# Repeated rows of step sizes and products, loaded per unit or per pair, in a hybrid Mamba kernel

## The chip, the core and the metric

The kernel runs on one NeuronCore of one Trainium2 chip. The core has five engines that run their own instruction queues in order: TensorE (PE, matrix products, with its weight loads shown as PEld), VectorE (DVE), ScalarE (ACT), GpSimd (POOL) and SyncE (SP). Here SP computes nothing: it issues most of the DMA transfers, one after another, and waits in front of each one until its buffer and its data are ready. The transfers themselves run on 16 DMA engines of the core. SBUF is the on-chip memory of 128 partitions; DRAM here is the chip's external memory.

The metric is the device time of one execution in microseconds (us). The kernel before has a median of 1525.69 us over 3 runs (1517.64 to 1526.01).

## What is computed

Eight sequences of 512 tokens with 256 channels pass four layers, each with a residual around it: a Mamba block with a feed-forward part, a gated recurrence over the 8 sequences, attention, and the same recurrence again. The change lies in the Mamba block, in its scan over time. Cut to that, the reference is:

```python
delta = jax.nn.softplus(dbc[..., :dt_rank] @ dt_proj_w + dt_proj_b)
Bm = dbc[..., dt_rank:dt_rank + N]
Cm = dbc[..., dt_rank + N:]
A = -jnp.exp(A_log)
deltaA = jnp.exp(delta[..., None] * A)
BX = (delta * xc)[..., None] * Bm[:, :, None, :]
def step(h, inp):
    dA, bx, c = inp
    h = dA * h + bx
    return (h, jnp.einsum('ben,bn->be', h, c))
```

Each of the 256 channels has 16 states (N). So the step sizes `delta` (called dl in the kernel) and the products `delta * xc` (called dx) are needed 16 times over, once for each state.

## The kernel before

**Tiling of the scan.** SBUF has 128 partitions. They are filled with 16 states times 8 channels; that is a *unit* (`scan_unit`, L403). 256 channels make 32 units for each sequence b, and 8 sequences make 256 units. A unit goes through these steps, each named in the order texts by a short word:

- `dl` and `dx` (`load_unit`, L374): the 8 rows of 512 floats are read from DRAM and written 16 times, once for each state, into one half of a tile `dl_rep` or `dx_rep` of 128 x 2 x 512. One DMA of 256 KB each, in pieces of one row, 2048 bytes. The two units u and u+1 (u even) share a tile; three such tiles exist for dl and three for dx.
- `da` (`decay`, L389): ACT computes exp(A * dl) for one unit into PSUM.
- `bx` (`increments`, L396): POOL multiplies dx by the repeated B, for a pair of units at once.
- `sc` (L405): DVE runs the scan over the 512 tokens. `cm` (L411): DVE multiplies by the repeated C.
- `y` (`sum_states`, L414): PE sums the 16 states of four units, one matmul for each, into the 32-row block j of a bank.

**Where the rows come from.** The step sizes of a sequence are computed by ACT into an SBUF tile `dl` of 128 x 2 x 512 (channel = 128 k + partition), the products by POOL into `dx` (piece `i.dx`, L328; for the first sequence by DVE in two halves). Pieces `i.store_dl` and `i.store_dx` (`store`, L330) write them to a DRAM tile of shape (k, partition, token), 512 KB each. For the first sequence each half k is stored by itself. All these DMAs are issued by SP (`nc.sync`). `i.rows` (L309) loads the repeated B and C, 256 KB each.

**Order.** All order is written out by hand. The texts `FRONT`, `SLOTS` (used 7 times, once for each step from one sequence to the next), `LAST` and `REST` list words; `mamba_and_recurrence` (L870) walks through them, and each word emits the next piece of its kind: `dl` the next load of a unit, `sc` the next scan and so on; `i.` pieces belong to the input side of the next sequence, `o.` to the output side of the previous one, `q.` and `r.` to the recurrence. Each engine then executes its part of the list strictly in that order. Around the stores, `SLOTS` reads (L831, L832):

```
cm sc cm cm cm sc sc cm y dx o.down3 o.down2 dl i.store_dl i.store_dx dx dl dl dx dl dx q.output0
i.rows dl q.g1 da e.square q.output0_ sc cm sc dx dx sc cm cm sc o.add3 cm cm o.add2 bx bx r.stats
```

The loads run ahead of their use by the three buffers: at the stores, the loads of units 0 to 28 of the running sequence are out for dl; those of 29 to 31 and the first ones of the next sequence follow the stores on SP's queue.

**Unit numbers.** Unit u has half k = u // 16, row block j = u % 4 and r = (u // 4) % 4; its channels start at 128 k + 32 j + 8 r. So the two units of a pair lie 32 channels apart.

Of the kernel before, what the change touches and what calls it, by code (L numbers as in the profile page):

```python
# [9 lines left out]
F32 = mybir.dt.float32  # L10
# [5 lines left out]
P = 128  # L16
B = 8
L = 512
E = 256
KC = E // P  # L20
TC = L // P
NS = 16
CG = P // NS
UNITS = E // CG
QR = 4
HC = 8
KCONV = 4
R = 64
# [108 lines left out]
def load_a(cx, w):  # L137
# [23 lines left out]

    a.sum = pool.tile([P, QR, HP], F32, name="sum")
    nc.gpsimd.memset(a.sum, 0.0)
    for r in range(QR):
        nc.vector.tensor_reduce(
# [12 lines left out]
def mamba_in(cx, a, t, b):  # L178

    nc, v = cx.nc, cx.v  # L180
    n = f"a{b}"
# [147 lines left out]

    def store(what, k):  # L330
        if not k:
            d = cx.dram.tile([KC, P, L], F32, tag=what, name=f"{what}_dram_{n}")
            setattr(t, what + "_d", d)
        to, x = (
            y[:, chunk(k), :]
            for y in (getattr(t, what + "_d").rearrange("k p l -> p k l"), getattr(t, what))
        )
        nc.sync.dma_start(to, x)

    def chunk(k):  # L340
        return slice(0, KC) if k is None else slice(k, k + 1)

    pieces = {
        f.__name__: f
        for f in (
            stats, rms, outer, residual, silu_z, silu_x, xproj, xproj_, rows, take_c,
        )
    }
# [3 lines left out]
    for k in (None, 0, 1):  # L352
        on = "" if k is None else f".{k}"
        pieces["dx" + on] = lambda k=k: times_input(k)
        for what in ("dl", "dx"):
            pieces[f"store_{what}{on}"] = lambda what=what, k=k: store(what, k)
        if on:
            pieces["silu_x" + on] = lambda k=k: silu_xk(k)
    for name, f, count in (("turn", turn, KC), ("proj", proj, 2 * KC), ("conv", conv, KC), ("dt", dt, KC)):
# [5 lines left out]
    return pieces  # L365


def unit_channels(u):


    return u // 16, u % 4, u // 4 % 4


def load_unit(cx, t, b, u, what):  # L374

    k, j, r = unit_channels(u)
    pair = getattr(t, what + "_rep")
    if u % 2 == 0:
        pair[u // 2] = cx.rep.tile(
            [P, 2, L], F32, tag=what, bufs=3, name=f"{what}_rep_a{b}_{u}"  # L380
        )
    c0 = j * HP + r * CG
    src = getattr(t, what + "_d")[k, c0 : c0 + CG, :]
    cx.nc.sync.dma_start(
        pair[u // 2][:, u % 2, :], src.unsqueeze(0).to_broadcast([NS, CG, L])
    )


def decay(cx, a, t, b, u):  # L389
# [13 lines left out]
def scan_unit(cx, t, b, u):  # L403
    t.hc[u] = cx.scan.tile([P, L], F32, tag="hc", bufs=HC, name=f"hc_a{b}_{u}")
    cx.nc.vector.tensor_tensor_scan(  # L405
# [8 lines left out]
def sum_states(cx, a, t, b, quad):  # L414

    k, r = quad // QR, quad % QR
    if r == 0:
        t.y[k] = cx.psum.tile([P, L], F32, tag="y", bufs=1, name=f"y_a{b}_{k}")
        cx.nc.tensor.matmul(t.y[k], a.D[:, k, :], t.xc[:, k, :], start=True, stop=False)
    for j in range(4):  # L420
        cx.nc.tensor.matmul(  # L421
            t.y[k][head(j), :],
            a.sum[:, r, :],
            t.hc[4 * quad + j],
            start=False,
            stop=(r == QR - 1),
        )
# [391 lines left out]


SLOTS = """
dx q.i0_ a.take_c y q.g0 sc o.gate1 cm i.rms x.load sc sc q.g0_ dl dl dl dx dl dl dl dx dx dx dx dx
dl dl dx dx dl dx dl dx dx dl da i.scale o.proj0 dx dx dl dx dl q.update0 dl dl o.proj1 i.turn0 q.f1
o.add_proj o.stats i.turn1 q.i1 da i.turn0_ q.f1_ sc i.turn1_ o.norm q.i1_ da cm cm cm q.hold1 y
o.turn0 bx bx e.stats bx bx bx o.residual c.bias bx bx bx o.turn1 o.turn0_ da sc sc o.turn1_ da
i.proj1 o.up0 o.up2 o.up1 da i.proj1_ o.up0_ da o.up2_ o.up1_ da da i.proj0 o.up3 o.up3_ i.proj0_ da
da e.center da sc cm sc cm i.conv1 cm sc da sc cm cm o.down1 y sc i.proj3 o.down0 x.half sc i.proj2
cm o.add1 i.conv0 sc cm sc cm i.silu_x i.silu_z y da i.xproj da i.xproj_ o.up4 dx dl dl dl dl dx dl
dx dx dx dx dl sc dl dx cm sc cm cm cm sc y i.dt1 sc o.add0 i.dt0 o.up5 o.up6 o.up7 da o.up4_ da
e.affine i.dt1_ i.dt0_ bx bx bx da i.dx da o.up5_ da o.up6_ da da o.up7_ da da e.outer da c.gate0 sc  # L830
cm sc cm cm cm sc sc cm y dx o.down3 o.down2 dl i.store_dl i.store_dx dx dl dl dx dl dx q.output0  # L831
i.rows dl q.g1 da e.square q.output0_ sc cm sc dx dx sc cm cm sc o.add3 cm cm o.add2 bx bx r.stats  # L832
bx e.residual sc sc q.g1_ r.norm cm cm q.update1 q.output1 y da r.turn0 y r.turn1 r.turn0_ da
r.turn1_ da r.f0 sc sc r.f0_ cm x.first sc r.i0 dl dl dx dl dx dl cm sc cm cm r.hold0 dx x.spill bx
da da q.output1_ bx dl dx da
"""


LAST = """
da dl dx dx q.i0_ da da dl dx dx sc y o.gate1 o.proj0 o.proj1 q.g0 dx dl dl dl dx x.spill dl dx dl  # L840
q.f1 dl dx dl dx dl x.load dx dx q.i1 dl dx dx sc sc o.add_proj bx o.stats a.take_c sc q.g0_ o.norm
sc q.f1_ da cm q.update0 sc cm q.hold1 cm cm dx dl dl dx dl dl dl dx dx dx dl dx dx dl dx dl dl dl
dl dx dx dx dl o.turn1 dl dx dl dl dx o.turn0 y o.turn1_ o.turn0_ bx bx bx o.up0 da da bx o.residual
bx bx bx bx o.up3 o.up1 bx o.up4 o.up2 q.i1_ da o.up0_ da da da q.output1_ o.up3_ o.up1_ da da da
o.up2_ q.output0_ da da o.up4_ da r.output0_ cm sc cm sc sc cm sc cm cm cm sc y sc cm cm y o.down0
o.down1 o.up6 o.up5 o.up7 o.up6_ da da o.up5_ da o.up7_ da da sc sc cm cm sc sc sc o.add0 o.add1 sc
# [15 lines left out]
i.stats i.outer i.center.a i.affine.a i.center.b i.affine.b i.square.a i.square.b i.residual i.rms  # L862
i.scale.a i.scale.b i.turn0 i.turn1 i.turn0_ i.turn1_ i.proj0 i.proj1 i.proj0_ i.proj1_ i.conv0
i.conv1 e.stats i.silu_x.0 i.silu_x.1 i.proj3 i.xproj i.xproj_ i.dt0 i.dt1 i.proj2 i.dt0_ i.dt1_
e.center i.dx.0 i.dx.1 i.rows e.affine i.store_dl.0 i.store_dx.0 i.store_dx.1 dl dx dx e.outer dl dl
da dx i.store_dl.1 e.square bx da da dx dl dx dx dl e.residual bx i.silu_z dx dl dx
"""


def mamba_and_recurrence(cx, a, w, d):  # L870
    nc = cx.nc
    T = [Ctx() for _ in range(B)]
    parts = {}
# [24 lines left out]

    parts["x", 0] = {"half": half_gates, "first": lambda: first_bias(cx, d.s)}
    for b in (1, 2, 3):  # L900
        parts["x", b + 1] = {"spill": lambda b=b: spill(b)}
    for b in (5, 6, 7):
        parts.setdefault(("x", b - 2), {})["load"] = lambda b=b: take_over(b)

    each = {
        "dl": (UNITS, lambda b, n: load_unit(cx, T[b], b, n, "dl")),
        "dx": (UNITS, lambda b, n: load_unit(cx, T[b], b, n, "dx")),
        "da": (UNITS, lambda b, n: decay(cx, a, T[b], b, n)),
        "bx": (UNITS // 2, lambda b, n: increments(cx, T[b], b, n)),
        "sc": (UNITS, lambda b, n: scan_unit(cx, T[b], b, n)),  # L910
        "cm": (UNITS, lambda b, n: times_c(cx, T[b], n)),
        "y": (UNITS // 4, lambda b, n: sum_states(cx, a, T[b], b, n)),
    }
    done = dict.fromkeys(each, 0)

    def run(b, one):
        if "." in one:
            who, what = one.split(".", 1)
            if (who, b) in parts and what in parts[who, b]:
                parts[who, b][what]()  # L920
        else:
            count, f = each[one]
            at, n = divmod(done[one], count)
            if at < B and (one != "y" or 4 * done[one] + 4 <= done["cm"]):
                f(at, n)
# [627 lines left out]
def lay_out(i):  # L1553
# [3 lines left out]
    i = {k: np.asarray(v) for k, v in i.items()}  # L1557
    A, F, T = "L0_attn_a_", "L0_ffn_", "L0_attn_b_"
# [32 lines left out]
    for h in range(H):  # L1591
        r = h % (2 * HG) * DH
        m = h % HG * HP
        watt[h // (2 * HG), r : r + DH, m : m + DH] = i[T + "w_att_val"][h]

    a_log = i[A + "A_log"].reshape(KC, 4, QR, CG, NS).transpose(4, 3, 0, 2, 1).reshape(P, UNITS)
    vecs = [a_log if name == "A_log" else cols(i[vec[name]]) for name, _ in _VECS]
    return {
        "x": i[A + "x"],
# [40 lines left out]
```

## Time and profile before

The execution that the profiler recorded took 1520.85 us; its span from the first to the last instruction is 1519.1 us. It lies between the lowest and the highest of the three timed runs.

| | busy us | share of the span |
|---|---|---|
| PE (matmul) | 1437.2 | 95% |
| PEld (weight load) | 702.1 | 46% |
| DVE | 1086.7 | 72% |
| ACT | 836.0 | 55% |
| POOL | 501.0 | 33% |

| stretch | what runs | granted PE clock | DMA share |
|---|---|---|---|
| 0 to 40 us | loads, input side of sequence 0 | 0.98 | 0.70 |
| 40 to 110 us | scans of sequence 0 | 0.82 | 1.02 |
| 110 to 190 us | scans of sequence 1 | 0.91 | 1.02 |
| 190 to 650 us | scans of sequences 2 to 7 | 1.00 | 0.87 to 1.01 |
| 650 to 1519 us | end of the recurrence, attention, second recurrence | 0.90 to 1.00 | 0.12 to 0.16 |

The DMA share is the mean busy share of the 16 DMA engines; it can come out a little over 1, because records of packets overlap slightly. The two kinds of repeated loads are the bulk of all traffic: 512 DMAs of 256 KB, 134 MB of the 197 MB moved. An engine's share over the span says little by itself: the engines have different limits in different stretches, and idle time of an engine that nobody waits for costs nothing.

### The profile page before, as it was taken

What the parts mean: (1) busy time and instruction counts of PE and PEld (TensorE: products, weight loads), DVE (VectorE), ACT (ScalarE), POOL (GpSimd) and SP (SyncE); (2) the same over time, 40 slices, a digit from 0 to 9 for tenths busy, and PEclk for the clock granted to TensorE, in tenths of its full rate; (3) what the DMA queues carried; (4) which work ended last, traced back from release to release, by engine and by line L of the source; (5) the groups of instructions that cost most, each with busy time, mean ns of one, the idle gap of its engine ahead of it and who ended that gap; (6) DMA issues with size and microseconds to landing.
All of it is one profiled execution on the core that took longest, in us unless ns stands there. A gap on an engine that the chain in (4) does not pass through costs nothing.

```text
span 1519.1 us, 19714 instructions
## 1 busy us (share of the span) xinstructions
PE 1437.2 (95%) x6812; PEld 702.1 (46%) x6812; DVE 1086.7 (72%) x1628; ACT 836.0 (55%) x1283; POOL 501.0 (33%) x300
## 2 busy tenths in 40 slices
PE   4479999999999999999899999999999999999998
PEld 1125455655555555667334443334333333333347
DVE  4799999999999899833766767565656646555326
ACT  5666778676867665522255464645455444554522
POOL 2777777776768566512300000000000000000000
PEclk9699999999999999999799999999999999999999
DMA  7999999899999999703101100100110001110214
GB/s 233 265 260 247 266 241 281 235 265 258 258 260 254 238 253 266 203 1 114 56 19 45 41 17 23 37 19 15 37 23 26 22 15 34 23 37 8 79 68 139
DMA packets 112141, 196.77 MB, mean 130 GB/s; under 512 B 17201, under 2 KB 27761, under 8 KB 112041
## 3 DMA queue, kind: packets, MB, share of 16 engines
q1 hardware_dynamic: 109752, 188.52, 46.7%
q10 hardware_dynamic: 1824, 5.15, 1.0%
q0 software_dynamic: 464, 1.84, 0.3%
q8 instruction: 54, 0.88, 0.2%
q14 instruction: 47, 0.38, 0.1%
HBM read 163.24 MB, written 23.56 MB: 123 GB/s over the span
## 4 chain that ended last, share of the span: by engine, by line
PE 82%; DVE 10%; ACT 3%; issue 2%; DMA 2%; POOL 1%; SPq 0%; ACTq 0%; DVEq 0%; POOLq 0%
PE ps_e_c L1104 10%; PE ps_s_c L1104 10%; PE ps_o_c L1124 8%; PE ps_f_o L522 6%; PE ps_f_o L498 6%; DVE hc_a L405 3%; PE y_a L421 3%; PE ps_in_a L245 3%; PE ps_w_c L1204 2%; PE ps_f_d L599 2%; PE ps_i_d L599 2%; PE ps_g_d L599 2%; DVE hc_a L411 2%; PE ps_v_c L1070 2%; PE ps_f_d L612 2%
## 5 line engine op out<-in xcount | busy, mean ns | idle before, releaser
L1386 DVE TENSOR_REDUCE mp<-ps_s_c 128x2 f32<-128x1024 f32 x256 | 305.5, 1222 | 174.0 <-PE ps_s_c L1104 125.5
L1403 ACT ACTIVATE e_c<-ps_e_c 128x1024 f32<-128x1024 f32 x256 | 255.2, 1022 | 221.3 <-PE ps_e_c L1104 146.4
L398 POOL TENSOR_TENSOR bx_a<-dx_rep_a,B_a 128x1024 f32<-128x1024 f32 x128 | 301.5, 2368 | 107.0 <-DMA dx_rep_a<-dx_dram_a 55.7
L405 DVE TENSOR_TENSOR_SCAN hc_a<-da_a,bx_a 128x512 f32<-128x512 f32 x256 | 304.6, 1214 | 20.2 <-POOL bx_a L398 9.6
L391 ACT ACTIVATE da_a<-dl_rep_a,neg_a 128x512 f32<-128x512 f32 x256 | 173.7, 688 | 113.9 <-DMA dl_rep_a<-dl_dram_a 64.3
L1104 PE MATMUL ps_e_c<-q_c,keys 32*128 32x512 f32 x1024 | 226.3, 630 | 0.7 <-DVE q_c L1395 0.7
L1104 PE MATMUL ps_s_c<-keys,q_c 32*128 32x512 f32 x1024 | 223.1, 649 | 3.0 <-DVE mp L1386 1.7
L411 DVE TENSOR_TENSOR hc_a<-hc_a,Cp_a 128x512 f32<-128x512 f32 x256 | 164.6, 674 | 0.0
L85 POOL TENSOR_TENSOR rs_d<-ve_d,neg_half 128x4 f32<-128x4 f32 x8 | 8.1, 1015 | 404.1 <-DVE ve_d L84 212.9
L1124 PE MATMUL ps_o_c<-e_c,va 128*32 128x512 f32 x1024 | 135.5, 607 | 0.0
L498 PE MATMUL ps_f_o<-h_o,w 128*128 128x256 f32 x512 | 116.6, 381 | 1.3 <-ACT f_o L511 0.8
L1104 PEld LDWEIGHTS ps_e_c<-q_c,keys 32*128 32x128 f32 x1024 | 68.5, 183 | 101.4 <-issue 52.9
L522 PE MATMUL ps_f_o<-w,f_o 128*128 128x256 f32 x512 | 115.1, 381 | 0.0
L498 PEld LDWEIGHTS ps_f_o<-h_o,w 128*128 128x128 f32 x512 | 96.2, 190 | 28.6 <-ACT da_a L391 6.8
L522 PEld LDWEIGHTS ps_f_o<-w,f_o 128*128 128x128 f32 x512 | 96.4, 190 | 22.1 <-ACT da_a L391 5.0
L421 PE MATMUL y_a<-hc_a,sum 128*32 128x512 f32 x512 | 90.1, 625 | 15.5 <-DVE hc_a L411 15.5
L1104 PEld LDWEIGHTS ps_s_c<-keys,q_c 32*128 32x128 f32 x1024 | 65.8, 187 | 72.5 <-issue 29.9
L85 POOL TENSOR_TENSOR rs_c<-ve_c,neg_half 128x4 f32<-128x4 f32 x7 | 7.1, 1010 | 217.6 <-DVE ve_c L84 217.6
L511 ACT ACTIVATE f_o<-ps_f_o,vecs 128x256 f32<-128x256 f32 x128 | 53.0, 467 | 23.4 <-PE ps_f_o L498 23.4
L245 PE MATMUL ps_in_a<-hT_a,w_in 128*128 128x512 f32 x128 | 65.0, 638 | 0.4 <-ACT dl_a L307 0.4
L1124 PEld LDWEIGHTS ps_o_c<-e_c,va 128*32 128x32 f32 x1024 | 21.6, 108 | 89.6 <-issue 87.1
L115 PE MATMUL ps_hT_a<-ident,h_a 128*128 128x128 f32 x64 | 13.4, 332 | 37.0 <-ACT h_a L225 35.9
(317 smaller groups left out, 1974.8 us busy)
## 6 DMA issues: line engine op xcount, KB each, us to landing
dl_rep_a<-dl_dram_a SPq DMA_DIRECT2D x256, 256.0 KB
dx_rep_a<-dx_dram_a SPq DMA_DIRECT2D x256, 256.0 KB
x<-in_x_dram SPq DMA_DIRECT2D x8, 512.0 KB
keys<-xT_c SPq DMA_DIRECT2D x128, 32.0 KB
o_c<-oT_c SPq DMA_DIRECT2D x128, 32.0 KB
xT_dram_d<-xT_d SPq DMA_DIRECT2D x8, 512.0 KB
xT_back<-xT_dram_d SPq DMA_DIRECT2D x8, 512.0 KB
sum_c<-inverse_c SPq DMA_DIRECT2D x15, 256.0 KB
```

Source lines behind the costliest of these rows:

```text
L245: nc.tensor.matmul(ps, a.in_proj[:, k, ts(m, P)], t.hT[:, k, :], start=(k == 0), stop=(k == KC - 1))
L391: cx.nc.scalar.activation(t.da[u], t.dl_rep[u // 2][:, u % 2, :], AF.Exp, scale=a.A[:, u : u + 1])
L398: cx.nc.gpsimd.tensor_mul(t.bx[pair], t.dx_rep[pair], t.B.unsqueeze(1).to_broadcast([P, 2, L]))
L405: cx.nc.vector.tensor_tensor_scan(t.hc[u], t.da[u], t.bx[u // 2][:, u % 2, :], 0.0, ALU.mult, ALU.add)
L411: cx.nc.vector.tensor_mul(t.hc[u], t.hc[u], t.Cp)
L421: cx.nc.tensor.matmul(t.y[k][head(j), :], a.sum[:, r, :], t.hc[4 * quad + j], start=False, stop=(r == QR - 1),)
L498: nc.tensor.matmul(ps[:, m, :], a.w1[:, k, ts(m0 + m, P)], t.h2[:, k, ts(half, L // 2)], start=(k == 0), stop=(k == KC - 1),)
L522: nc.tensor.matmul(ps, t.f[c // 2][:, m, ts(c % 2, P)], a.w2[:, m, :], start=(m == 0), stop=(m == FC - 1),)
L1104: cx.nc.tensor.matmul(ps[:, j, :], lhs[rows, :], rhs[rows, :], start=True, stop=True)
L1124: cx.nc.tensor.matmul(po[head(j), :], c.va[b % 2][:, t, g * HG + j, :], es[j // 2][:, j % 2, :], start=(t == 0), stop=(t == TC - 1),)
L1386: nc.vector.tensor_reduce(c.mp[:, t, h : h + 2, DH], ps.pop(("s", b, g, t, i)), AX.X, ALU.max, negate=True)
L1403: nc.scalar.activation(e, ps.pop(("e", b, g, t, i)), AF.Exp)
```

## The change

The DRAM tiles get the shape (k, 64, 2, token): row c of half k holds channel c and channel c + 64, one behind the other, 4096 bytes. A store now writes one half k, from 128 partitions to a view (2, 64, token) of that half; the store of both halves at once is gone, so each sequence has four stores of 256 KB in place of two of 512 KB. `load_pair` takes the place of `load_unit`: one DMA of 512 KB fills a whole tile of a pair, 16 copies of 8 rows of 4096 bytes. For that, the two units of a pair have to be 64 channels apart; `QUAD` swaps the middle two of the four row blocks, both in `sum_states` and in the layout of `A_log`. In the order texts, each `dl` and `dx` is now a pair: `FRONT` has 3 and 4 in place of 6 and 8, `SLOTS` 16 and 16 in place of 32 and 32, `LAST` 13 and 13 in place of 26 and 26. No arithmetic is changed.

```diff
     def store(what, k):
         if not k:
-            d = cx.dram.tile([KC, P, L], F32, tag=what, name=f"{what}_dram_{n}")
+            d = cx.dram.tile([KC, P // 2, 2, L], F32, tag=what, name=f"{what}_dram_{n}")
             setattr(t, what + "_d", d)
-        to, x = (
-            y[:, chunk(k), :]
-            for y in (getattr(t, what + "_d").rearrange("k p l -> p k l"), getattr(t, what))
-        )
-        nc.sync.dma_start(to, x)
+        to = getattr(t, what + "_d")[k].rearrange("c h l -> h c l")
+        nc.sync.dma_start(to, getattr(t, what)[:, k, :])
...
-def load_unit(cx, t, b, u, what):
-
-    k, j, r = unit_channels(u)
-    pair = getattr(t, what + "_rep")
-    if u % 2 == 0:
-        pair[u // 2] = cx.rep.tile(
-            [P, 2, L], F32, tag=what, bufs=3, name=f"{what}_rep_a{b}_{u}"
-        )
+def load_pair(cx, t, b, pair, what):
+
+    k, r, j = pair // 8, pair // 2 % QR, pair % 2
+    rep = cx.rep.tile([P, 2, L], F32, tag=what, bufs=3, name=f"{what}_rep_a{b}_{2 * pair}")
+    getattr(t, what + "_rep")[pair] = rep
     c0 = j * HP + r * CG
-    src = getattr(t, what + "_d")[k, c0 : c0 + CG, :]
-    cx.nc.sync.dma_start(
-        pair[u // 2][:, u % 2, :], src.unsqueeze(0).to_broadcast([NS, CG, L])
-    )
+    src = getattr(t, what + "_d")[k, c0 : c0 + CG]
+    cx.nc.sync.dma_start(rep, src.unsqueeze(0).to_broadcast([NS, CG, 2, L]))
...
-            t.y[k][head(j), :],
+            t.y[k][head(QUAD[j]), :],
...
-cm sc cm cm cm sc sc cm y dx o.down3 o.down2 dl i.store_dl i.store_dx dx dl dl dx dl dx q.output0
-i.rows dl q.g1 da e.square q.output0_ sc cm sc dx dx sc cm cm sc o.add3 cm cm o.add2 bx bx r.stats
+cm sc cm cm cm sc sc cm y dx o.down3 o.down2 dl i.store_dl.0 i.store_dl.1 i.store_dx.0 i.store_dx.1 dl dx q.output0
+i.rows dl q.g1 da e.square q.output0_ sc cm sc dx sc cm cm sc o.add3 cm cm o.add2 bx bx r.stats
...
-e.center i.dx.0 i.dx.1 i.rows e.affine i.store_dl.0 i.store_dx.0 i.store_dx.1 dl dx dx e.outer dl dl
-da dx i.store_dl.1 e.square bx da da dx dl dx dx dl e.residual bx i.silu_z dx dl dx
+e.center i.dx.0 i.dx.1 i.rows e.affine i.store_dl.0 i.store_dx.0 i.store_dx.1 dl dx e.outer dl
+da dx i.store_dl.1 e.square bx da da dx dl e.residual bx i.silu_z dx
```

In the new `SLOTS` the `dl` in front of the stores is the pair of units 28 and 29, the `dl` behind them the pair of units 30 and 31, the last of the running sequence; the `dx` after it is the first pair of the next sequence.

More of the change, by code (lines that the diff above doesn't have):

```diff
@@ L25 @@
 QR = 4
+QUAD = (0, 2, 1, 3)
 HC = 8
@@ L354, in mamba_in @@
         pieces["dx" + on] = lambda k=k: times_input(k)
-        for what in ("dl", "dx"):
-            pieces[f"store_{what}{on}"] = lambda what=what, k=k: store(what, k)
+        if on:
+            for what in ("dl", "dx"):
+                pieces[f"store_{what}{on}"] = lambda what=what, k=k: store(what, k)
         if on:
@@ L365, in mamba_in @@
     return pieces
-def unit_channels(u):
-    return u // 16, u % 4, u // 4 % 4
-def load_unit(cx, t, b, u, what):
-    k, j, r = unit_channels(u)
-    pair = getattr(t, what + "_rep")
-    if u % 2 == 0:
-        pair[u // 2] = cx.rep.tile(
-            [P, 2, L], F32, tag=what, bufs=3, name=f"{what}_rep_a{b}_{u}"
-        )
+def load_pair(cx, t, b, pair, what):
+    k, r, j = pair // 8, pair // 2 % QR, pair % 2
+    rep = cx.rep.tile([P, 2, L], F32, tag=what, bufs=3, name=f"{what}_rep_a{b}_{2 * pair}")
+    getattr(t, what + "_rep")[pair] = rep
     c0 = j * HP + r * CG
-    src = getattr(t, what + "_d")[k, c0 : c0 + CG, :]
-    cx.nc.sync.dma_start(
-        pair[u // 2][:, u % 2, :], src.unsqueeze(0).to_broadcast([NS, CG, L])
-    )
+    src = getattr(t, what + "_d")[k, c0 : c0 + CG]
+    cx.nc.sync.dma_start(rep, src.unsqueeze(0).to_broadcast([NS, CG, 2, L]))
 def decay(cx, a, t, b, u):
@@ L821 @@
 SLOTS = """
-dx q.i0_ a.take_c y q.g0 sc o.gate1 cm i.rms x.load sc sc q.g0_ dl dl dl dx dl dl dl dx dx dx dx dx
-dl dl dx dx dl dx dl dx dx dl da i.scale o.proj0 dx dx dl dx dl q.update0 dl dl o.proj1 i.turn0 q.f1
+dx q.i0_ a.take_c y q.g0 sc o.gate1 cm i.rms x.load sc sc q.g0_ dl dl dl dx dx dx
+dl dx dl dx dl da i.scale o.proj0 dx dx dl q.update0 dl o.proj1 i.turn0 q.f1
 o.add_proj o.stats i.turn1 q.i1 da i.turn0_ q.f1_ sc i.turn1_ o.norm q.i1_ da cm cm cm q.hold1 y
@@ L827 @@
 da e.center da sc cm sc cm i.conv1 cm sc da sc cm cm o.down1 y sc i.proj3 o.down0 x.half sc i.proj2
-cm o.add1 i.conv0 sc cm sc cm i.silu_x i.silu_z y da i.xproj da i.xproj_ o.up4 dx dl dl dl dl dx dl
-dx dx dx dx dl sc dl dx cm sc cm cm cm sc y i.dt1 sc o.add0 i.dt0 o.up5 o.up6 o.up7 da o.up4_ da
+cm o.add1 i.conv0 sc cm sc cm i.silu_x i.silu_z y da i.xproj da i.xproj_ o.up4 dl dl dx
+dx dx dl sc cm sc cm cm cm sc y i.dt1 sc o.add0 i.dt0 o.up5 o.up6 o.up7 da o.up4_ da
 e.affine i.dt1_ i.dt0_ bx bx bx da i.dx da o.up5_ da o.up6_ da da o.up7_ da da e.outer da c.gate0 sc
-cm sc cm cm cm sc sc cm y dx o.down3 o.down2 dl i.store_dl i.store_dx dx dl dl dx dl dx q.output0
-i.rows dl q.g1 da e.square q.output0_ sc cm sc dx dx sc cm cm sc o.add3 cm cm o.add2 bx bx r.stats
+cm sc cm cm cm sc sc cm y dx o.down3 o.down2 dl i.store_dl.0 i.store_dl.1 i.store_dx.0 i.store_dx.1 dl dx q.output0
+i.rows dl q.g1 da e.square q.output0_ sc cm sc dx sc cm cm sc o.add3 cm cm o.add2 bx bx r.stats
 bx e.residual sc sc q.g1_ r.norm cm cm q.update1 q.output1 y da r.turn0 y r.turn1 r.turn0_ da
-r.turn1_ da r.f0 sc sc r.f0_ cm x.first sc r.i0 dl dl dx dl dx dl cm sc cm cm r.hold0 dx x.spill bx
-da da q.output1_ bx dl dx da
+r.turn1_ da r.f0 sc sc r.f0_ cm x.first sc r.i0 dl dx dl cm sc cm cm r.hold0 dx x.spill bx
+da da q.output1_ bx da
 """
 LAST = """
[L840 to L843, printed above, removed]
+da dl dx q.i0_ da da dx sc y o.gate1 o.proj0 o.proj1 q.g0 dx dl dl x.spill dx dl
+q.f1 dl dx x.load dx q.i1 dl dx sc sc o.add_proj bx o.stats a.take_c sc q.g0_ o.norm
+sc q.f1_ da cm q.update0 sc cm q.hold1 cm cm dl dx dl dx dl dx dx dl dl
+dx dl o.turn1 dx dl o.turn0 y o.turn1_ o.turn0_ bx bx bx o.up0 da da bx o.residual
 bx bx bx bx o.up3 o.up1 bx o.up4 o.up2 q.i1_ da o.up0_ da da da q.output1_ o.up3_ o.up1_ da da da
@@ L905, in mamba_and_recurrence @@
     each = {
-        "dl": (UNITS, lambda b, n: load_unit(cx, T[b], b, n, "dl")),
-        "dx": (UNITS, lambda b, n: load_unit(cx, T[b], b, n, "dx")),
+        "dl": (UNITS // 2, lambda b, n: load_pair(cx, T[b], b, n, "dl")),
+        "dx": (UNITS // 2, lambda b, n: load_pair(cx, T[b], b, n, "dx")),
         "da": (UNITS, lambda b, n: decay(cx, a, T[b], b, n)),
@@ L1594, in lay_out @@
         watt[h // (2 * HG), r : r + DH, m : m + DH] = i[T + "w_att_val"][h]
-    a_log = i[A + "A_log"].reshape(KC, 4, QR, CG, NS).transpose(4, 3, 0, 2, 1).reshape(P, UNITS)
+    a_log = i[A + "A_log"].reshape(KC, 4, QR, CG, NS)[:, QUAD, :, :, :]
+    a_log = a_log.transpose(4, 3, 0, 2, 1).reshape(P, UNITS)
     vecs = [a_log if name == "A_log" else cols(i[vec[name]]) for name, _ in _VECS]
```

## The prediction

> **What bounds the kernel now.** I read first the busy times by stretch, then the chain of waits, then the waits by engine, and last single stretches for the pace of the DMA engines.
>
> Busy times in the two stretches of the scan (columns: length; busy us of PE, PEld, DVE, ACT, POOL with instruction counts; granted clock; DMA share; GB/s):
>
> ```profile
> 215.00:590.00 375.00, 372.24 (x1498) 217.57 (x1497) 355.58 (x549) 265.57 (x468) 265.77 (x138) 1.00 0.98 257
> 40.00:215.00 175.00, 139.12 (x487) 67.79 (x488) 164.97 (x248) 118.72 (x209) 134.08 (x71) 0.89 1.01 257
> ```
>
> From 215 us on PE is idle for under 3 of 375 us, at full clock; DVE is busy for 95%. Before, DVE has 94% and PE is idle for a fifth. The DMA engines are full in both, but being full is not being waited for. The chain of waits (start, us, what) shows who is:
>
> ```profile
> 334.39 0.59 PE ps_xT_b L115 x4
> 334.98 1.00 PE y_a L421 x8
> 335.98 0.58 PE ps_xT_b L115 x4
> 336.56 1.80 PE ps_f_b L599 x4
> 338.36 1.72 PE ps_f_b L612 x4
> ```
>
> It runs through PE alone here, without a gap; the matmuls of line 522, one in each step, start at 241.46 and 319.41, so a step takes 77.9 us. Waits for the repeated loads exist (total us, times, longest, 190 to 570 us):
>
> ```profile
> POOL bx_a L398 <- DMA dx_rep_a<-dx_dram_a: 41.0, 16, 6.3
> ACT da_a L391 <- DMA dl_rep_a<-dl_dram_a: 22.2, 17, 2.6
> ```
>
> but POOL and ACT are busy for 71% and absorb nearly all of it. In the scan's whole chain after the start only two DMA pieces of note stand, 5.79 us at 170.43 and 6.23 us at 548.33. So a faster load has at most 12 us to win there. A slower transfer has no such limit: the DMA engines have no reserve.
>
> **The pace of the DMA engines**, from four stretches (columns as above):
>
> ```profile
> 186.00:200.00 14.00, 12.94 (x49) 6.80 (x48) 13.93 (x26) 8.74 (x15) 6.66 (x4) 1.00 1.06 269
> 247.20:249.80 2.60, 2.60 (x14) 2.29 (x13) 2.60 (x8) 2.31 (x8) 2.60 (x2) 1.00 1.04 403
> 985.00:985.80 0.80, 0.80 (x10) 0.58 (x12) 0.80 (x2) 0.80 (x1) 0.00 (x0) 1.00 1.00 410
> 886.00:886.40 0.40, 0.40 (x5) 0.31 (x8) 0.21 (x1) 0.00 (x0) 0.00 (x0) 1.00 0.59 215
> ```
>
> First row, only repeated loads: 16 pieces of 2048 bytes at 269 GB/s are 122 ns, times the share 1.06 = 129 ns of an engine for each piece. Second row, the stores of dl and dx, also in 2048-byte pieces: 81 ns x 1.04 = 85 ns. Third row, a store in 4096-byte pieces: 160 ns. So a piece costs some 10 ns and 75 ns for each 2048 bytes, and the repeated loads cost 44 ns more. They are slow because of what they read (16 engines read the same eight rows at once), not because of the chip's load: the stores in the midst of them go at full pace. Fourth row, a load of the attention's repeated sums, whose DRAM side has an outermost count of 8: half the bytes per time at half the share. The trace's records of single packets there show 8 packets started every 80 ns, and 16 in the others. A DMA with 8 blocks outermost ran on 8 engines.
>
> **The loads.** One DMA with 8 pieces of 4096 bytes for each engine replaces two with 8 of 2048. No row shows a repeated load in 4096-byte pieces. Lower bound: the plain piece, 160 ns; upper bound: no gain, 2 x 129 = 258 ns. I take the middle, 210, since a penalty could go by pieces or by bytes and no row is nearer to one. A pair then takes 1.7 us (1.3 to 2.1) in place of 2.1. Since the loads are behind PE, I book only what stands in the chain: the two pieces, 12.0 us, are mostly queues of such loads; a queue shortens by at most 38%, so -4.6 us (0 to -12). SP issues 32 loads fewer in a step, 0.5 to 0.6 us each, and four stores for two; SP spends its time waiting for buffers (98 us for POOL's bx), so this is booked at nothing. A pair has to be free as a whole; it had to before, since both units share a tile. `QUAD` and `A_log` change addresses only: nothing.
>
> **The stores.** This is where I see the cost. Before, the DRAM view of a store starts with 128 partitions: 512 pieces of dl and dx spread over 16 engines, 32 x 85 ns = 2.7 us for both (the second row above). Now the view is (2, 64, 512): two blocks outermost. By the row with 8 blocks on 8 engines, these DMAs run on 2 engines. Then each store is 64 pieces for each of the two, 64 x 85 ns = 5.4 us, and the four of a sequence 21.7 us one after the other. Bounds: 2.7 us, if they spread after all, and 64 x 4 x 129 ns = 33 us, if they go at the slow pace. I take 21.7: a store has many sources and never showed the slow pace.
>
> [...]
>
> All loads behind the stores need all 16 engines, and each engine works its SP queue in order. What waits is seen in the order on SP and ACT at the fourth step:
>
> ```profile
> 321.80 0.59 SPq L338 DMA_DIRECT2D dl_dram_a<-dl_a  x1
> 322.91 0.36 SPq L338 DMA_DIRECT2D dx_dram_a<-dx_a  x1
> ```
>
> ```profile
> 335.02 0.58 ACT L661 COPY xT_b<-ps_xT_b 128x512 f32<-128x512 f32 x1
> 335.50 0.70 ACT L391 ACTIVATE da_a<-dl_rep_a,neg_a 128x512 f32<-128x512 f32 x1
> 336.60 0.58 ACT L661 COPY xT_b<-ps_xT_b 128x512 f32<-128x512 f32 x1 [0.40 <-PE ps_xT_b L115]
> ```
>
> The ACT row at 335.50 is `da` of unit 30. Its pair is loaded by the `dl` right behind the four stores. In the seven steps unit 30 is wanted 11.5, 11.0, 11.6, 13.7, 10.5, 11.3 and 10.5 us after the first store is issued: mean 11.4. The pair lands after: issue 0.6, 0.8 until data and receipt (an isolated repeated load: issued by 39.9, landed 41.81, of which about 1.05 is transfer), 1.0 for a load still ahead, 21.7 for the stores, 1.7 for itself: 25.8. So ACT waits 14.4 us at unit 30. Behind it in ACT's queue stands the second copy of xT (336.60), on which PE's next matmuls (336.56 in the chain) wait: PE stops too. DVE lacks the scan of unit 30. Nothing recovers this, since PE has no idle time afterwards. The next sequence's first dx pair, B, C and dl pair are queued behind; at 1.7 us for a pair they land by +32, and are wanted (POOL at 336.83, DVE's Cp at 341.93, `da` at 340.70) at +15 to +20 plus the 14.4: no second stop. Seven steps: 7 x 14.4 = 101 us.
>
> At the start the same happens once, on this chain:
>
> ```profile
> 35.09 3.61 DMA dl_dram_a<-dl_a
> 39.94 1.87 DMA dx_rep_a<-dx_dram_a
> 44.51 2.33 POOL bx_a L398
> ```
>
> Data of B and C end at about 37.0; dl.0, dx.0 and dx.1 then take 3 x 5.4 on the two engines, to 53.2. The first dl pair lands at about 55.4, the first dx pair at 57.1, where POOL began its bx at 44.51: +12.6 us.
>
> Sum: 1520.85 + 101 + 12.6 - 4.6 = 1629.9, about 1630 us on the profiled execution, which is 4.8 us (0.3%) under the median of the runs.
>
> **Rivals.**
>
> A, the forecast: two engines, stops of 10 to 18 us in each step: 1595 to 1660. Chance 0.76.
>
> B, slower still: DMA-bound. An engine's time in a step is 0.98 x 77.9 = 76.3; less 512 x 129 ns of loads and 2.7 of stores that leaves 7.5 for the rest. The two engines would then carry 256 pieces + 21.7 + 7.5: 70 at 160 ns, 95 at 258 ns. A step under A takes 92.3, so only at the upper end do they set the step: 95 gives 1520.85 + 7 x 17.3 + 12.6 = 1654; with stores at the slow pace as well, 106 gives 1731. For it: the penalty may go by bytes. Chance 0.10.
>
> C, not slower: the stores spread over 16 engines, or at least 4. With k engines they take 43.4/k us; at 4 this is 10.9, and the pair lands at +15, late by some 3.6 us at most; at 16 nothing is late. Then only the gain is left: 1516 us, at best 1509 with both DMA pieces gone. Against it: the row with 8 blocks. Chance 0.14. Of it I put 0.04 at a gain over 1%, since the chain offers no more than 12 of 1521 us, 0.08 within 1%, and 0.02 slower (k = 4).
>
> **How the numbers follow.** 1630 is the likeliest case; alone it would range from 1595 to 1660. The range for 8 in 10 leaves out C, and the far end of B: 1575 to 1685; the lower end is A with stops of 6 us. The three runs before spread by 0.55%, so I count 1% as no change. Slower by over 1%: 0.76 + 0.10 + 0.02 = 0.88; same 0.08; faster 0.04.
>
> **What will show it.** In the profile after, ACT's longest wait for `dl_rep_a` is 10 us or more, seven times, right after the stores; the DMA share falls to near 0.13 (2 of 16) for some 20 us in each step; PE idles there; the step takes about 92 us; the first bx starts near 57. If the stores land within 4 us of their issue, C holds. If the DMA share never falls and the step is still longer, B. A pair's load should run at 270 to 410 GB/s. I am wrong if PE's chain stays unbroken from 215 to 590.

## The result, and the profile after

The changed kernel takes 1689.53 us (median of 4 runs, 1688.03 to 1690.99). The kernel before, run beside it, takes 1525.47 us (4 runs, 1517.64 to 1526.01). The ratio is 1.109, with a 95% interval of 1.105 to 1.113: slower, as forecast, but 4.5 us beyond the upper end of the range, and 59.5 us over the forecast.

Busy times in the same two stretches of the scan as before (columns: length; busy us of PE, PEld, DVE, ACT, POOL with instruction counts; granted clock; DMA share; GB/s), and a third row from inside one step, behind its four stores:

```profile
40.00:215.00 175.00, 111.38 (x360) 52.50 (x360) 127.35 (x177) 88.11 (x150) 106.78 (x53) 0.78 0.84 203
215.00:590.00 375.00, 301.24 (x1144) 172.34 (x1145) 279.80 (x443) 212.29 (x383) 211.17 (x115) 0.89 0.81 198
```

```profile
413.50:424.50 11.00, 8.46 (x39) 3.65 (x37) 6.88 (x9) 6.76 (x17) 5.08 (x4) 1.00 0.13 52
```

From 215 us on, PE is now idle for 74 of 375 us (before: under 3), and no engine is near full. The DMA share fell from 0.98 to 0.81. The third row says where the share went: for 11 us it stands at 0.13, which is 2 of 16. In it the records of single packets (one for each piece) show 25 pieces of 2048 bytes each us, of 84 ns each, which is 2.1 engines' worth of work. The stores run on two engines. They are the same two for all stores that are queued there: all four are issued by 419.84, yet two packets are under way for 9.5 of these 11 us and three for 1.5.

The chain of waits in the fourth step (start, us, what), where before PE ran without a gap:

```profile
373.54 10.14 DMA dx_rep_a<-dx_dram_a
...
395.31 6.84 DMA dx_rep_a<-dx_dram_a
...
405.29 8.62 DMA dl_rep_a<-dl_dram_a
...
419.94 15.47 DMA dl_rep_a<-dl_dram_a
...
435.50 0.69 ACT da_a L379
436.19 0.52 ACT xT_b L649
...
436.75 2.07 PE ps_f_b L587 x2
438.83 3.41 PE ps_f_b L600 x4
```

The piece of 15.47 us is the stop that was forecast: the pair of unit 30, then its `da` on ACT, then the copy of xT behind it in ACT's queue, then PE. The first three pieces were not forecast. They are repeated loads that come late: two far from the stores, and the third is the load issued right in front of them. The last two lines also show PE after the stop: the four matmuls of line 600 (612 before) take 3.41 us instead of 1.72, at a granted clock of 0.50 from 436.8 to 442.2.

The issuing side of the same moment (start, us, engine, line, operation; in brackets the idle time before and what ended it):

```profile
405.90 1.45 SPq L336 DMA_DIRECT2D dl_dram_a<-dl_a  x2
407.39 12.45 SPq L336 DMA_DIRECT2D dx_dram_a<-dx_a  x2
419.94 4.93 SPq L374 DMA_DIRECT2D dl_rep_a<-dl_dram_a  x1
428.21 0.56 SPq L374 DMA_DIRECT2D dx_rep_a<-dx_dram_a  x1
435.50 0.69 ACT L379 ACTIVATE da_a<-dl_rep_a,neg_a 128x512 f32<-128x512 f32 x1 [14.64 <-DMA dl_rep_a<-dl_dram_a]
```

ACT's stop is 14.64 us here. SP itself is held: it needs 12.45 us to issue the two stores of dx and 4.93 for the next load, where such an issue took 0.4 to 0.6 us before. From 407.39 to 428.21 us SP issues nothing but these.

The waits by engine, 190 to 570 us (total us, times, longest):

```profile
ACT da_a L379 <- DMA dl_rep_a<-dl_dram_a: 103.7, 23, 15.6
POOL bx_a L386 <- DMA B_a<-bc_a: 80.0, 4, 20.5
```

ACT's wait for `dl_rep_a` rose from 22.2 to 103.7 us, and POOL has a new one, 20 us at the first `bx` of a sequence, for the B that is issued behind the stores and behind the late load. The first stores of the seven steps are issued at 117.55, 209.86, 305.71, 405.90, 506.39, 606.96 and 707.27: the steps grow from 92.3 to 95.9 and then to 100.2 to 100.6 us. Before, they were 71.1 to 81.0, on average 76.4.

The start, on the changed kernel's chain (start, us, what):

```profile
41.70 16.18 issue
57.91 2.34 POOL bx_a L386
```

The first `bx` begins at 57.91; 57.1 was forecast. The first `da` begins at 56.01; its pair was forecast to land at 55.4.

So two things have to be told apart: the stop behind the stores, and whatever makes the rest of a step late. The records of packets name a suspect: in steady steps (306 to 706 us) a piece of 4096 bytes, nearly all of them of repeated loads, takes 277 ns on average (quartiles 249 and 313). A piece of 2048 took 128 ns there before. The forecast took 210 for the large one, with 160 and 258 as bounds.

### The profile page after: what moved, and what is told of

Read it like the earlier page. It is cut to its first block, busy times and chain, and to the rows that moved or that the text cites. A ratio compares the mean times of both kernels' runs of the same rounds, so it can differ in the third digit from the quotient of the medians.

```text
span 1689.1 us, 19281 instructions
## 1 busy us (share of the span) xinstructions
PE 1466.6 (87%) x6812; PEld 713.5 (42%) x6812; DVE 1090.9 (65%) x1628; ACT 834.3 (49%) x1283; POOL 500.2 (30%) x300
## 4 chain that ended last, share of the span: by engine, by line
PE 57%; DMA 21%; POOL 7%; DVE 6%; ACT 5%; issue 3%; SPq 1%; ACTq 0%; POOLq 0%; DVEq 0%
DMA dl_rep_a<-dl_dram_a 12%; PE ps_e_c L1092 9%; PE ps_s_c L1092 9%; PE ps_o_c L1112 7%; DMA dx_rep_a<-dx_dram_a 5%; POOL bx_a L386 4%; DMA dx_dram_a<-dx_a 4%; PE ps_w_c L1192 2%; PE ps_f_d L587 2%; DVE hc_a L393 2%; PE ps_i_d L587 2%; PE ps_g_d L587 2%; PE ps_v_c L1058 2%; PE ps_f_d L600 1%; PE ps_o_b L1281 1%
## 5 line engine op out<-in xcount | busy, mean ns | idle before, releaser
L393 DVE TENSOR_TENSOR_SCAN hc_a<-da_a,bx_a 128x512 f32<-128x512 f32 x256 | 305.4, 1212 | 162.3 <-issue 92.3
L486 PE MATMUL ps_f_o<-h_o,w 128*128 128x256 f32 x512 | 122.8, 394 | 10.8 <-ACT f_o L499 8.6
L409 PE MATMUL y_a<-hc_a,sum 128*32 128x512 f32 x512 | 95.4, 648 | 32.6 <-DVE hc_a L399 32.6
L1092 PEld LDWEIGHTS ps_e_c<-q_c,keys 32*128 32x128 f32 x1024 | 68.3, 183 | 100.6 <-issue 52.9
L587 PE MATMUL ps_f_b<-xT_b,gw 128*128 128x512 f32 x56 | 34.8, 732 | 85.0 <-ACT xT_b L649 84.8
```

What stands on the lines that cost most here:

```text
L393: cx.nc.vector.tensor_tensor_scan(t.hc[u], t.da[u], t.bx[u // 2][:, u % 2, :], 0.0, ALU.mult, ALU.add)
L409: cx.nc.tensor.matmul(t.y[k][head(QUAD[j]), :], a.sum[:, r, :], t.hc[4 * quad + j], start=False, stop=(r == QR - 1),)
L486: nc.tensor.matmul(ps[:, m, :], a.w1[:, k, ts(m0 + m, P)], t.h2[:, k, ts(half, L // 2)], start=(k == 0), stop=(k == KC - 1),)
L587: cx.nc.tensor.matmul(ps[:, tk], cx.gw[:, g, k, ts(m, P)], xT[:, k, tk], start=(k == 0), stop=(whole and k == KC - 1),)
L1092: cx.nc.tensor.matmul(ps[:, j, :], lhs[rows, :], rhs[rows, :], start=True, stop=True)
```

## The experiments

**One part at a time.** Three kernels separate the two parts of the change: the form of the stores and the size of the loads' pieces. All keep the pairwise layout in DRAM. The kernel before, run again beside each group of experiments, had medians of 1520 to 1526 us; each ratio is against the median of its own group, and differences in us between kernels of different groups are good to some 6 us.

The first spreads the stores: it cuts each by the two blocks of 64 channels, so that 64 rows stand outermost.

```diff
-        to = getattr(t, what + "_d")[k].rearrange("c h l -> h c l")
-        nc.sync.dma_start(to, getattr(t, what)[:, k, :])
+        for h in range(2):
+            to = getattr(t, what + "_d")[k][:, h, :]
+            nc.sync.dma_start(to, getattr(t, what)[h * P // 2 : (h + 1) * P // 2, k, :])
```

> The changed kernel with each store cut in two, one for each block of 64 channels, so that no side has 2 outermost; the loads stay in 4096-byte pieces. Theory 1 (two causes that add on the same two DMA engines: the stores on 2 engines, 21.7 us a step, and 256 repeated pieces of 4096 bytes at about 285 ns, 73 us, with 7.5 us of other traffic: 102 us, measured step 100.4): the stops behind the stores go, an engine keeps 73 + 2.7 + 7.5 = 83 us of work, the step falls from 100 to about 83 and stays above the 77.9 of before; time 1545 to 1570 us. Theory 2 (the stops behind the stores are the whole loss, the piece size costs nothing on the path): step 77.9, time 1513 to 1529 us. Theory 3 (the coarser loads by pairs cost by themselves, the stores little): time above 1600 us.

Measured: 1564.31 us, ratio 1.028 (1.026 to 1.030). The two-engine form of the stores costs 125 of the 164 us, and the large loads cost the other 39. In the busy times and the chain of this kernel it is seen how:

```profile
215.00:590.00 375.00, 360.11 (x1426) 211.80 (x1425) 333.86 (x512) 255.70 (x453) 252.28 (x132) 0.98 0.98 238
```

```profile
382.37 6.34 DMA dx_rep_a<-dx_dram_a
...
391.83 8.37 DMA dl_rep_a<-dl_dram_a
...
414.23 7.29 DMA dx_rep_a<-dx_dram_a
...
424.64 7.13 DMA dl_rep_a<-dl_dram_a
```

The share is 0.98 as before the change, but the bytes per time fell from 257 to 238 GB/s, and repeated loads now stand in the chain four times in 50 us. All 16 engines are full and now waited for. Steady steps take 82.5 to 84.1 us.

The second keeps the stores on two engines and fills each pair by two loads of 2048-byte pieces.

```diff
-    cx.nc.sync.dma_start(rep, src.unsqueeze(0).to_broadcast([NS, CG, 2, L]))
+    for h in range(2):
+        cx.nc.sync.dma_start(rep[:, h, :], src[:, h, :].unsqueeze(0).to_broadcast([NS, CG, L]))
```

> The changed kernel with each pair loaded by two DMAs in 2048-byte pieces, from the same DRAM layout; the stores stay on two engines. Theory 1: an engine's step is 512 x 129 ns = 66, plus 21.7, plus 7.5 = 95 us, against 102; time 1640 to 1668 us. Theory 2: the stops stay as they are and nothing else was lost, 1680 to 1697 us. Theory 3: near the time before, 1520 to 1540 us.

Measured: 1649.52 us, ratio 1.084 (1.083 to 1.086), steps of 92.8 us on average. Its chain has the forecast stop (`dl_rep_a`, then `da`, xT and PE):

```profile
396.44 14.34 DMA dl_rep_a<-dl_dram_a
...
410.87 0.69 ACT da_a L380
411.56 0.52 ACT xT_b L650
...
412.12 2.08 PE ps_f_b L588 x2
```

The third has both edits, so of the change only the layout, `QUAD` and the shorter texts are left.

> Both of the edits above together: spread stores and 2048-byte pieces; what is left of the change is the layout in DRAM with the rows of one unit 4096 bytes apart, the pairing by 64 channels and the order by pairs. Theories 1 and 2: the time before, 1513 to 1530 us. Theory 3: clearly above it, over 1550 us. If rows 4096 bytes apart were themselves slow to read, over 1530 us too, which the pace run tells apart.

Measured: 1525.55 us (median of 10 runs) against 1520.12 (13 runs), ratio 1.003 (1.002 to 1.004): no change by the 1% bound. Its row from 215 to 590 us reads nearly as before the change, with a DMA share of 0.95 instead of 0.98:

```profile
215.00:590.00 375.00, 372.28 (x1501) 218.65 (x1500) 355.94 (x549) 264.14 (x466) 266.63 (x139) 1.00 0.95 257
```

The four kernels make a square. The large loads cost 38.8 us with spread stores (1564.3 - 1525.5) and 40.0 with stores on two engines (1689.5 - 1649.5); the stores cost 124.0 with small loads and 125.2 with large ones. The two costs add up. The layout by itself costs 0.2 to 0.4%, which is under the bound of 1%.

**What one piece costs.** A kernel with DMAs alone measures each kind of transfer in a row of its own: repeated loads of 1024, 2048 and 4096-byte pieces, plain ones, stores in both forms. No computation of the kernel is left in it.

> No computation of the reference is left: only DMAs on SP, in groups of 8 MB with gaps between, each of one kind: repeated 2048-byte pieces from 8 adjacent rows, repeated 4096-byte pieces, repeated 2048-byte pieces from rows 4096 bytes apart, repeated 1024-byte pieces, 2048-byte and 4096-byte pieces where each partition has its own row, the first two again, then 4 of the changed kernel's 256 KB stores in each of two forms. Theory 1: the repeated 4096-byte piece is slow by itself: 270 to 300 ns against 125 to 132 for 2048 bytes, with every engine idle; its own rows run at 160 and 85 ns. If the slowness came from the kernel around it (other traffic, the queues' order), it takes 160 to 258 ns here. Stores with 2 outermost: 64 pieces of 84 ns on each of two engines, about 5.4 us each, one after the other; in the other form 8 pieces on each of 16, under 1 us each.

Measured, from the packets: a repeated piece of 2048 bytes takes 107 to 117 ns the first time and 126 to 133 when the same group is repeated later; one of 4096 bytes takes 209 to 230 and 270 to 284. So the pace drifts within one execution, and the large piece takes 1.9 to 2.2 times the small one early and late. Pieces of 1024 bytes take 50 to 64 ns. A larger repeated piece saved nothing for each byte. Plain rows take 85 to 88 and 163 to 165 ns, and the two-engine stores 84 ns, as in the forecast.

**The order of the loads.** If only the stop behind the stores counts, then the last `dl` of the running sequence put in front of the stores should remove it. In `SLOTS`:

```diff
-o.down2 dl i.store_dl.0 i.store_dl.1 i.store_dx.0 i.store_dx.1 dl dx q.output0
+o.down2 dl dl i.store_dl.0 i.store_dl.1 i.store_dx.0 i.store_dx.1 dx q.output0
```

> The changed kernel with one word moved in the order text: the load of the last dl pair of the running sequence stands in front of the four stores in place of behind them. Theory 1a (with 4096-byte pieces the two loaded DMA engines, 102 us of work in a step, set the step, whatever waits first): almost unchanged, 1678 to 1696 us. Theory 1b (the stop of ACT at unit 30 is what adds to the step): the next thing wanted from behind the stores is the first dx pair of the next sequence, some 4 to 6 us later, so the step falls by that; 1645 to 1662 us.

Measured: 1680.72 us, ratio 1.105 (1.100 to 1.110). The stop only moved. The chain of waits now runs through the stores of dx themselves (20.87 us): SP issues the next sequence's first load when they have landed, and behind it the load of dl that ACT then waits for:

```profile
405.04 20.87 DMA dx_dram_a<-dx_a
...
427.93 9.81 DMA dl_rep_a<-dl_dram_a
```

The same move on the kernel with small loads:

> The kernel with stores on two engines and 2048-byte pieces (1649.5 us), with the same word moved: the last dl pair is loaded in front of the stores. There the two engines have 95 us of work for a step of 95, but the chain of waits runs over PE without a break from one stop to the next. Theory 1b (stop plus PE's own time): each stop falls by 4 to 6 us, 1607 to 1622 us. Theory 1a (the two engines set the step): 1640 to 1655 us.

Measured: 1639.76 us, ratio 1.076 (1.072 to 1.080), just under what 1a expects. Again the stop moved, to the C of the next sequence:

```profile
387.33 18.38 DMA dx_dram_a<-dx_a
...
407.74 6.16 DMA C_a<-bc_a
```

**The place of the stores.** Here the second store of dl and of dx goes to the end of a step's text, so that two stores instead of four stand in front of the loads.

```diff
-o.down2 dl i.store_dl.0 i.store_dl.1 i.store_dx.0 i.store_dx.1 dl dx q.output0
+o.down2 dl i.store_dl.0 i.store_dx.0 dl dx q.output0
...
-da da q.output1_ bx da
+da da q.output1_ bx da i.store_dl.1 i.store_dx.1
```

> The changed kernel with the second of the two stores of dl and the second of the two stores of dx moved to the end of a step's schedule; the first of each stays where it was. Theory 1a (two engines carry more work in a step than a step lasts, so the place of the stores matters little): 1680 to 1695 us, steps of about 100 us as now. Theory 1b (it is the burst of four stores in front of the wanted loads that stops the engines): the burst is halved, the stop at da falls to under 6 us, 1595 to 1645 us.

> The kernel that stores pairwise on two engines but loads each pair with two loads of 2048-byte pieces (1649.5 us), with the second store of dl and of dx moved to the end of a step's schedule. Theory 1a (the two engines' work sets the step): 1635 to 1655 us. Theory 1b (the burst in front of wanted loads sets it, since the two engines have 256 small pairs' worth of loads at about 65 to 70 us and 29 us of stores, about 95 us a step, only just more than the others need): 1530 to 1590 us.

Measured: 1668.75 us, ratio 1.093 (1.090 to 1.095), with large loads, and 1629.48, ratio 1.068 (1.066 to 1.070), with small ones. Both lie between the two theories, nearer to 1a. With large loads the longest stop at `da` was 14.6 to 18.7 us in each of the seven steps and is now 5.4 to 9.5, yet the step shrinks only from 98.3 to 95.2 us on average. The stop's length and the step's length do not go together; the place of the stores is worth 21 and 20 us of the 125 and 124.

**Half of the stores.** The stores of dx are spread as in the first experiment, those of dl stay on two engines.

```diff
-        to = getattr(t, what + "_d")[k].rearrange("c h l -> h c l")
-        nc.sync.dma_start(to, getattr(t, what)[:, k, :])
+        if what == "dl":
+            to = t.dl_d[k].rearrange("c h l -> h c l")
+            nc.sync.dma_start(to, t.dl[:, k, :])
+            return
+        for h in range(2):
+            to = t.dx_d[k][:, h, :]
+            nc.sync.dma_start(to, t.dx[h * P // 2 : (h + 1) * P // 2, k, :])
```

> The changed kernel with the stores of dx cut by halves of 64 channels, so that they spread over 16 engines; the stores of dl stay in the form that runs on two. The loads stay in 4096-byte pieces. Without two-engine stores this was 1564 us with steps of about 83.4 us, with both it is 1689.5 with steps of about 100. Theory 1a (two engines' own work sets the step): 256 pieces at 285 ns, 10.9 us of dl stores, 1.4 of dx, 7.5 of the rest are about 92.8 us a step, 1620 to 1640 us in all, half of the way. Theory 1b (only the stop at da counts): 10.8 us less in front of the load of unit 30 leaves a stop of some 4 us, and the total is 1564 and seven of these and some 6 at the start: 1590 to 1605 us.

Measured: 1618.3 us, ratio 1.063 (1.060 to 1.066), just under 1a's interval and 13 us over 1b's. Steady steps take 87.8 to 89.1 us, which lies between 1a's 92.8 and the 87.4 of a stop of 4 us on top of 83.4. Half of the two-engine stores cost 54 of 125 us. By itself this run decides little; it fits a cost that goes nearly by the amount of work on the two engines.

**Why repeated pieces are slow.** Two kernels of loads alone (no computation of the kernel is left) vary the source of 128 destination rows. In the first, each next group of 8 rows starts `step` rows further on, from 0 (repeated) to 8 (all rows their own, one unbroken walk):

```python
src = bass.AP(x, first * l, [[step * l, NS], [l, CG], [1, l]])
```

> No computation of the reference is left: only groups of loads of 8 MB from the input in DRAM, in which DMA engine s starts at row first + s * step and takes 8 rows. Steps 0, 1, 4, 8 and 0 again with rows of 2048 bytes, then 0, 1, 4 and 0 again with rows of 4096 bytes. Step 0 is the repeated load of the kernels, step 8 gives every engine its own rows. Theory A (the repeated loads are slow because 16 engines read the same row at the same time): steps 1 and 4 run at the pace of step 8, 84 to 88 ns and 160 to 165 ns, and step 0 at 110 to 130 and 213 to 285. Theory B (they are slow because few bytes of DRAM serve all, in whatever order): step 1 as slow as step 0, step 4 between. Theory C (a repeated 4096-byte piece pays the penalty by bytes): step 0 with 4096 at 1.9 to 2.2 times step 0 with 2048.

Measured, as the mean of a group's pieces: for 2048 bytes 133 ns at step 0, 130 at 1, 122 at 4, 94 at 8 (86 to 92 within the group) and 123 at 0 again; for 4096 bytes 284 at 0, 284 at 1, 284 at 4 and 283 at 0 again. Rows in common at the same moment are not the reason, if each group of 8 rows has an engine of its own; this is the author's reading, since the records name no engine.

The second keeps the three-level form also for rows of their own (step 9), changes the order, and has one group that reads one row for all:

```python
src = bass.AP(x, first * l, [[step * l, NS], [row * l, CG], [1, l]])
```

> Only loads, no computation, nine groups of 8 MB, each of 128 destination rows; what differs is the source: rows of 2048 bytes, of their own and in order; repeated for eight destination rows; of their own but interleaved; in the other order of repetition (neighbouring destination rows alike); one row for all; repeated rows far apart; then rows of 4096 bytes, of their own, repeated, and in the other order. Theory D (the three-level form of the source is what is slow, repetition or not): rows of their own in that form take as long as repeated ones, 125 to 135 ns for 2048 bytes and about 280 for 4096. Theory E (it is the repetition, the same bytes of DRAM asked for by several engines): rows of their own take 84 to 92 ns and 160 to 170 ns in any form, and one row for all is the slowest.

Five of its nine groups in busy times by stretch (length; busy us of DVE and POOL with instruction counts; granted clock; DMA share; GB/s; 16 engines x piece / rate x share is the time of a piece): 2048 bytes of their own, repeated, one row for all, then 4096 bytes of their own, repeated.

```profile
8.00:32.00 24.00, 18.88 (x218) 7.01 (x8) 1.00 1.05 280
38.00:62.00 24.00, 18.86 (x124) 0.00 (x0) 1.00 1.05 278
134.00:154.00 20.00, 10.22 (x69) 0.00 (x0) 1.00 1.02 160
214.00:236.00 22.00, 12.16 (x120) 0.00 (x0) 1.00 1.03 292
244.00:266.00 22.00, 11.08 (x115) 0.00 (x0) 1.00 1.03 283
```

Rows of their own (280 GB/s) are as slow as repeated ones (278); by the packets of a whole group 121 and 123 ns, and 234 and 237 for 4096 bytes. The other four groups lie beside them: 125 ns interleaved, 125 in the other order, 114 for repeated rows far apart, and 232 for 4096 bytes in the other order. Theory E falls, but for its last clause: one row for all is slower still, 160 GB/s or 209 ns in the stretch shown, 183 ns over its whole group. Theory D is right in its order and wrong in its level for 4096 bytes: 234 ns was measured, 280 expected, and the level drifts. What in the form makes it slow (16 walks through DRAM side by side, or the form of the description itself) is left open; no run here separates these.

## What in the prediction was right, and which step failed

**The bound and the sign.** Right in the sign. PE's chain was unbroken before, and the DMA engines, at a share of 0.98 to 1.01 in the scan, had no reserve for slower transfers. That little was left to gain from faster loads is not shown: no run here has any. The kernel that has only the layout, the pairing and the order changed (1.002 to 1.004) shows that they cost at most 0.4%.

**The stores on two engines.** Right, and shown in the share of 0.13 and the 84 ns for a piece. The forecast carried one row, a load with 8 blocks outermost at a share of 0.59, over to stores with 2. None of its rows shows a store of that form, so this step was the author's estimate; so was the sum of 21.7 us, which has all four stores on the same two engines, one after the other. The trace after agrees for a store with 2 blocks (52 GB/s at a share of 0.13), and with two packets under way for 9.5 of 11 us it agrees on the same two. That an engine takes SP's transfers in their order is seen at the load of unit 30's pair: 112 of its 128 pieces, 14 x 8, start from 425.66 to 428.02 us, while the stores go on at 25 pieces each us, and it lands only at 435.41. What counts other than these give is not shown. Cutting the same stores so that 64 stands outermost brought back 125 us.

**The stop and the start.** Right in size: 14.4 us forecast at `da` of unit 30, and 14.6 to 18.7 us found once in each of the seven steps (15.9 on average); the first `bx` was forecast at 57.1 and came at 57.91. The terms for the two-engine stores, 101 + 12.6 = 113.6 us, stand against 124 to 125 measured.

**"No second stop".** Wrong in its reason. The forecast counted what the two engines still owe and let SP issue on. But SP's issue itself stood still for 12.45 and 4.93 us and then for up to 3.4 more until the stores of dx had landed, so the next sequence's dx, B and C were issued only afterwards, and POOL waited for B for up to 20.5 us between 190 and 570. Moving the load of unit 30 ahead of the stores gave back only 9 to 10 us (with large loads the intervals of the two ratios overlap), since the next items stopped in its place. SP's issue, which the forecast booked at nothing, was part of the path.

**The loads.** This is the step that failed: "I take the middle, 210", between 160 and 258 ns, booked as a gain of 4.6 us. Measured in the kernel: 277 ns, beyond the upper bound, since the penalty went by the byte and somewhat more (277 / 128 = 2.2); a pair's load ran at 237 GB/s, where 270 to 410 had been named as a sign. The square of four kernels prices this part at +39 to +40 us. The gain was also booked against the forecast's own price: 4.6 us is the 38% of a piece of 160 ns, and at 210 it would be 19%, 2.2 us. And the reason given for the slow loads, 16 engines that read the same eight rows at once, is wrong: rows of their own in the same three-level form took as long (121 ns against 123). With spread stores, an engine's step is 256 x 277 ns = 71, stores of 512 / 16 = 32 pieces at the 85 ns of before = 2.7, and the 7.5 us of the rest: 81 us by this estimate, which is more than the 77.9 of PE. The first experiment's steady steps, 82.5 to 84.1 us, lie 1 to 3 us above it. So the large loads by themselves turned a PE-bound scan into a DMA-bound one.

**Rival B.** With 277 in place of 210, the forecast's own sum for the two engines is 71 + 21.7 + 7.5 = 100.2 us in a step. Measured: 100.2 to 100.6 in the steady steps. Put into the formula of rival B it gives 1520.85 + 7 x (100.2 - 77.9) + 12.6 = 1689.6; measured 1689.5. The agreement to the microsecond is luck, since the first two steps are shorter, the steps before were 76.4 on average, and the sum itself is a little too large, as the last lines of this paragraph show. The mechanism is supported by the runs: moving the stores or the load leaves most of the cost in place, and half of the stores costs 43% of it. Its limits show too. The sums for the kernel with half the stores (71 + 10.9 + 1.4 + 7.5 = 91) and for the one with small loads (512 x 120 ns = 61, + 21.7 + 7.5 = 91; the 120 are 16 x 2048 bytes / 211 GB/s x 0.77 from 215 to 590 us) stand against steady steps of 88 to 89 and 94 to 96. In the second the stop of 14.34 us, which holds ACT and PE, probably counts as well. The records name the queue of a packet and not its engine, so the work of the two cannot be read directly; but how many packets are under way at a moment can be counted. In each steady step of the changed kernel it is 16 or more for 71 to 74 us, exactly two for 14 to 15, and fewer than two for 3 to 6. With spread stores it is 16 or more for 74 to 76 us and exactly two for under 1. So the time in which only two engines work comes on top of the time in which all do, and at least one of the two stands still for 3 to 6 us of a step: they set most of the step, not all of it. No run issues the stores from another engine's queue, so the part of SP's held issue in the 124 to 125 us is not separated from the work on the two engines.

**The miss in numbers.** Of the 59.6 us between 1629.9 and 1689.5, the loads make 43 (38.8 instead of -4.6), the stores 11 (125.2 instead of 113.6), and 4.8 is the distance of the profiled execution from the median, which the forecast had noted. The range ended at 1685 because it held case A and left out the far end of B. B had been given a chance of 0.10, since its condition, 258 ns, was taken as the far end of the price.

## What to carry to other kernels

Here the outermost count of a DMA's view went with the engines that worked on it: a load with 8 blocks had a share of 0.59, the stores with 2 one of 0.13, and with 64 outermost the time on two engines alone fell from 14 to 15 us in a step to under 1. If a layout is changed, look at the outermost count of every transfer that touches it, the stores too, not only those that were meant to become faster. Where the DMA engines are full but not waited for, a transfer's price per byte is the number to measure before pieces are merged; fewer and larger pieces helped nothing here, because twice the bytes took 2.2 times the time (277 ns against 128). When some engines get extra work, add up the work of those engines alone in a step, and compare the sum with the step; where it is the larger, a stop that is taken away in one place can move to another: here the load put in front of the stores gave back only 9 to 10 us.

## What the runs showed that was not expected

- Slow transfers held back the queue that issued them: the two stores of dx, 256 KB each on two engines, took 11.5 to 12.8 us to issue in the seven steps, and the load behind them 4.93 us in the fourth, against 0.4 to 0.6 us for an issue before. It is not only the two engines: with spread stores, four issues of dx took 4.1 to 5.9 us beside large loads and 2.5 to 2.9 beside small ones.
- The pace of repeated loads is not constant: 107 to 117 ns and then 126 to 133 for the same pieces of 2048 bytes within one execution, and 209 to 230 and then 270 to 284 for 4096. What moves it was not found.
- Loads need not repeat rows to be slow: rows of their own in the same three-level form took 121 ns against 123, while an unbroken walk took 86 to 92. One row for all took 183 over its whole group.
- After the stop in the fourth step PE resumed at a granted clock of 0.50 (436.8 to 442.2 us), so that four matmuls took 3.41 us instead of 1.72: the stop cost PE more than its length.
